# Seed stage of a two-layer network: three segments in turn instead of one, and no constant products

## The chip, the cores and the metric

The kernel runs on one core of a Trainium2 chip. The metric is device time in microseconds (us) for the whole program, from the first to the last instruction; lower is better. Times of before: 18684.27, 18656.47 and 18677.33 us, median 18677.33 us.

A core has five instruction queues that run side by side, each in its own order: TensorE (PE, matrix products into PSUM), VectorE (DVE), ScalarE (ACT, functions such as exp and silu), GpSimd (POOL) and SyncE (SP, which issues the transfers here). They meet only at semaphores: an instruction waits until what it reads is written and what it overwrites is read.

## The reference, cut to what matters

The reference is a network of two layers on 8 images of 128 channels and 64x64 points (L = 4096 points in a row). The change touches one part of the second layer: how `seed` comes from the layer's input.

```python
# per image; x is the first layer's result with the expert output added (x2 below)
v    = _ln_c(x)                                   # centre and scale over the channels
g    = einsum(v, seed_tok_w) + seed_tok_b         # 128 channels -> 8
gf   = _mamba(g.T, sm_in_w, in_b, conv_w, conv_b, A_log, D, dt_bias, rms_w, out_w, headdim=8, d_state=16) + g.T
seed = v + einsum(gf, seed_detok_w) + seed_detok_b
# _mamba: z, x, B, C, dt from one projection, a 3-tap convolution and silu;
# decay exp(cumsum(dt*A)) between any two points of a chunk; a state S handed from chunk to chunk;
# y*silu(z), divided by its root mean square, times out_w
```

The same normalised values, normalised once more, go to the other branch (`xs`), which the stage after this one (`cascade`) reads.

## The kernel before, in words

The program has, one after another, the first layer (until about 8.8 ms), its experts, a setup, the seed stage (`seeds`, L1457, from about 9.36 to 10.30 ms), the cascade (to about 17.1 ms) and the last feed-forward part. The seed stage alone is touched. The 8 images are worked together: their 8 x 8 tokens lie side by side on the partitions.

**Input units.** `seed_inputs` (L1359) is a generator with 64 units, one for each of 8 stretches of 512 points and 8 images. A unit goes through four steps, one at each `next`: `residual` (product `x2_p`, shown as `x_p` in the profile, then an addition and a store), `center` (product `ln_m`, a subtraction, a square), `scales` (product `ln_v`, three ACT functions, two DVE products, a store to `seed`) and `outputs` (two ACT functions, product `tok_p`, a store to `g_d`, a store to `xs`). So each `next` issues four products for four different units. All four take one of two PSUM banks with the tag "p".

**Segments.** The 4096 points are cut into 16 segments of 256 (SC). `seed_segment` (L1428) takes one through, with yields where other work may be put between:

- `tap_stack` (L1314) loads three shifted copies of `g_d` into one of two stacks `stk_sm`.
- `ssd_project` (L1079): products `bc_p`, `z_p`, `tok_p`; their silus on ACT between two loads of function tables; then softplus for dt, and in `ssd_exponents` (L1050) the cumulative-sum product `cs_p`, whose result is split in three bf16 parts, written to DRAM (`cs_sm`) and read back in 16 small transfers into the rows `ssA`, `ssB`; last `dec_p`, `cd_p` and `eA_p`.
- `ssd_chunk` (L1173), for each of two chunks of 128 points: `g_p`, masked into `gm`; two halves, each with four products `ss_p` of the rows, an exp into `E`, a DVE product with `gm`, and `y_p`; and the state S.
- `ssd_output` (L1291): square, product `ms_p`, Ln and exp, a POOL product, product `o_p`. Then `gf`, and for each image a product `det_p` (tag "p" again), a DVE addition `sd_x` and a store.

In the profile nearly all instructions have the line of a helper (L288 products, L296 ACT, L335 and L344 DVE or POOL), so names of tiles are followed, not lines. Products of the segment's own token projection are shown as `tok_p<-W_sm,stk_sm`, those of a unit as `tok_p<-xn,w_seeds`.

**Order.** `seeds` (L1473 to L1478) takes the segments one by one. It first draws enough units that the segment's stretch is in `g_d`, and then calls `next(ready)` once at every fourth yield of the segment, which has 20. Across the queues a scheduling layer of the language sets, when the program is built, the final order of each engine's instructions; it may move an instruction ahead of others as long as the data allow, and dependencies given by `self.after` hold as well. [...]

**Constant products.** `keep_warm` (L290) multiplies a constant tile by itself into a bank that the next product overwrites. Six of them stand ahead of `cs_p` (L1058) and six ahead of `ms_p` (L1300) in every segment of the seed stage; the cascade has none.

Of the kernel before, what the change touches and what calls it, by code (L numbers as in the profile page):

```python
# [9 lines left out]
F32 = mybir.dt.float32  # L10
BF16 = mybir.dt.bfloat16
AF = mybir.ActivationFunctionType
ALU = mybir.AluOpType
# [7 lines left out]
NB = 8  # L21
C = 128
# [256 lines left out]
class Net:  # L279
# [709 lines left out]
    def ssd_weights(self, pool, cfg, j):  # L989

        nc = self.nc
        n = f"{cfg.name}{j}"

        def part(i):
            o, m = self.at["stacked"][f"{n}_{i}"]
            return self.st[:, o : o + m]

        W = pool.tile([128, cfg.cols], F32, name=f"W_{n}")
        nc.vector.memset(W[96:], 0.0)
        self.tt(W[:KST], part(0), part(1), ALU.mult)  # L1000
        self.tt(W[:KST], W[:KST], part(2), ALU.add)
        negA = pool.tile([128, cfg.nh], F32, name=f"negA_{n}")
        self.act(negA, self.w(f"{n}_Alog"), AF.Exp)
        self.ts(negA, negA, -1.0, ALU.mult)
        D = pool.tile([128, cfg.g2, cfg.nh, cfg.hd], F32, name=f"D_{n}")
        for g in range(cfg.g2):
            nc.vector.tensor_copy(D[:, g], bc(self.w(f"{n}_D"), cfg.hd))
        wo = pool.tile([cfg.pz, cfg.gh * cfg.co], F32, name=f"wo_{n}")
        self.ts(wo, self.w(f"{n}_out")[: cfg.pz], self.w(f"{n}_rms")[: cfg.pz], ALU.mult)
        return {"W": W, "negA": negA, "D": D.rearrange("p g h q -> p (g h q)"), "wo": wo, "fill": 6 if cfg is SM else 0}  # L1010

    def ssd_rings(self, pool, cfg, n, npads, nrows, nstates):

        nc = self.nc
        pads = []
        for q in range(npads):
            t = pool.tile([128, cfg.g, cfg.pad], F32, name=f"pad_{cfg.name}{q}")
            nc.vector.memset(t, 0.0)  # L1020
            pads.append(t)
        ncs = n // 128 * (cfg.g // cfg.g4)
        rows_ = []
        for q in range(nrows):
            A = pool.tile([128, ncs, cfg.g4, 128], BF16, name=f"ssA_{cfg.name}{q}")
            for c in range(ncs):
                nc.vector.tensor_copy(A[:, c], bc(self.k("ss_one")[:, : cfg.g4], 128))
            B = pool.tile([128, ncs, cfg.nh, 128], BF16, name=f"ssB_{cfg.name}{q}")
            for c in range(ncs):
                nc.vector.tensor_copy(B[:, c], bc(self.k(f"ss_ind_{cfg.name}"), 128))  # L1030
            rows_.append((A, B))
        states = []
        for q in range(nstates):
            t = pool.tile([cfg.pb, cfg.np, cfg.g2 * cfg.hi], F32, name=f"Sd_{cfg.name}{q}")
            nc.vector.memset(t, 0.0)
            states.append(t)
        stacks = []
        for q in range(2):
            t = pool.tile([128, cfg.np, n], F32, name=f"stk_{cfg.name}{q}")
            nc.vector.memset(t[96:], 0.0)  # L1040
            stacks.append(t)
        return {"pads": pads, "rows": rows_, "states": states, "stacks": stacks,
                "pad": 0, "row": 0, "state": 0, "stack": 0}
# [6 lines left out]
    def ssd_exponents(self, cfg, dA, n_tok, ring, wk, ps, fill):  # L1050


        nc = self.nc
        NC, nh, G = n_tok // 128, cfg.nh, cfg.g
        n = NC * G * nh
        t_ = cfg.name
        p = ps.tile([128, S], F32, tag="b", bufs=self.narrow, name="cs_p")
        self.keep_warm(p, fill)  # L1058
        p = p[:n, :128]
        self.summed = self.mm(p, dA.rearrange("p c g -> p (c g)"), self.k("le"))  # L1060
        part = wk.tile([n, 3, 128], BF16, name=f"csq_{t_}")
        rest = wk.tile([n, 128], F32, name=f"csr_{t_}")
        nc.vector.tensor_copy(part[:, 0], p)
        self.tt(rest, p, part[:, 0], ALU.subtract)
        nc.vector.tensor_copy(part[:, 1], rest)
        self.tt(part[:, 2], rest, part[:, 1], ALU.subtract)
        d = self.dp.tile([3, n, 128], BF16, name=f"cs_{t_}", bufs=3)
        nc.sync.dma_start(d.rearrange("i n t -> n i t"), part)
        A, B = self.turn(ring, "row")
        g4 = cfg.g4  # L1070
        for r in range(g4):
            v = d.rearrange("i (c g h) t -> i c g h t", g=g4, h=nh)[:, :, r]
            nc.sync.dma_start(B[32 * r : 32 * r + 3], v)
            for i in range(3):
                o = 32 * r + 3 + i * nh
                nc.sync.dma_start(A[o : o + nh, :, r], v[i].rearrange("c h t -> h c t"))
        return A, B, part
# [213 lines left out]
    def ssd_output(self, cfg, W, sg, n_tok, wk, ps):  # L1291

        nc = self.nc
        NH, gh, pz, t_ = cfg.nhalf, cfg.gh, cfg.pz, cfg.name
        yz = sg["yz"]
        sq = wk.tile([pz, NH, n_tok], F32, name=f"sq_{t_}", bufs=1)
        self.act(sq, yz, AF.Square)
        yield None
        p = ps.tile([128, 2, S], F32, tag="a", bufs=self.wide, name="ms_p")
        self.keep_warm(p[:, 0], 6 if cfg is SM else 0)  # L1300
        for hf in range(NH):
            self.mm(p[:pz, hf, :n_tok], self.k(f"blk_{t_}")[:pz, :pz], sq[:, hf])
        self.rsqrt(sq, p[:pz, :NH, :n_tok], self.k("e5")[:pz])
        self.tt(yz, yz, sq, ALU.mult, nc.gpsimd)
        yield None
        o = ps.tile([128, S], F32, tag="b", bufs=self.narrow, name="o_p")
        n = gh * cfg.co
        for hf in range(NH):
            i = self.mm(o[hf * n : (hf + 1) * n, :n_tok], W["wo"], yz[:, hf])
            if cfg is CM and hf == 0:  # L1310
                self.after(i, self.projected)
        yield o[: NH * n, :n_tok]
# [46 lines left out]
    def seed_inputs(self, g_d, routed, wk, ps):  # L1359
# [16 lines left out]

        def residual(s, b, v):
            p = bank("x2_p")
            self.mm(p, self.eo[:, b, :], v["P"])
            self.tt(v["x"], v["x"], p, ALU.add)  # L1380
            nc.sync.dma_start(self.x2[b][:, v["sg"]], v["x"])

# [42 lines left out]
            made.pop(t - len(steps), None)  # L1425
            yield t - len(steps)

    def seed_segment(self, k, g_d, st, wk, ps):  # L1428

        nc = self.nc  # L1430
        sg = slice(k * SC, (k + 1) * SC)
        stk = self.tap_stack(g_d, k * SC, k == 0, st["ring"])
        xs = []
        for b in range(NB):
            x = wk.tile([C, SC], F32, name="sd_x", bufs=NB)
            nc.sync.dma_start(x, self.seed[b][:, sg])
            xs.append(x)
        for v in self.ssd_project(SM, self.ssw[2], st["ring"], lambda j: stk[:, j, :], SC, wk, ps):
            if v == "silu" or isinstance(v, dict):
                yield  # L1440
        for c in range(SC // 128):
            yield from self.ssd_chunk(SM, self.ssw[2], st, v, c, wk, ps)
        for o in self.ssd_output(SM, self.ssw[2], v, SC, wk, ps):
            if o is None:
                yield
        gf = self.gf[k % 2]
        for j in range(SM.np):
            self.tt(gf[32 * j : 32 * j + 32], o[32 * j : 32 * j + 32], stk[64:96, j, :], ALU.add)
        for b, x in enumerate(xs):
            p = ps.tile([C, S], F32, tag="p", bufs=2, name="det_p")  # L1450
            self.mm(p[:, :SC], self.w(f"detok_w{b}"), gf)
            self.stt(x, p[:, :SC], self.w("seed_detok_b"), x, ALU.add, ALU.add)
            nc.sync.dma_start(self.seed[b][:, sg], x)
            if b % 2:
                yield

    def seeds(self):  # L1457

        nc, tc = self.nc, self.tc
        with tc.tile_pool(name="sd", bufs=1) as pl, tc.tile_pool(name="sdw", bufs=2) as wk, \  # L1460
# [2 lines left out]
            self.weights(pl, "seeds")  # L1463
            self.silus_done([])
            g_d = self.dp.tile([8 * NB, L], F32, name="g_d")
            st = {"ring": self.ssd_rings(pl, SM, SC, 2, 2, 2), "S": None, "layer": 0}
            routed = [pl.tile([128, S], F32, name=f"P{q}") for q in range(3)]
            self.gf = [pl.tile([128, SC], F32, name=f"gf{q}") for q in range(2)]
            for z in routed + self.gf:
                nc.vector.memset(z[64:], 0.0)  # L1470
            ready = self.seed_inputs(g_d, routed, wk, ps)
            done = -1
            for k in range(NSC):  # L1473
                while done < (k * SC // S + 1) * NB - 1:
                    done = next(ready)
                for n, _ in enumerate(self.seed_segment(k, g_d, st, wk, ps)):
                    if n % 4 == 0:
                        done = next(ready, done)  # L1478
            self.wname, self.wt = second

    def cascade(self, ps):
# [410 lines left out]
```

## Time and profile before

| | us |
|---|---|
| median of three runs | 18677.33 |
| the profiled execution, time | 18687.58 |
| its span | 18685.8 |
| seed stage, first cumulative-sum product | 9441 |
| end of the part of the seed stage with input units | 10079 |
| last cumulative-sum product of the stage | 10256 |
| last `sd_x` addition of the stage | 10297 |

A row of the view by stretches gives, for each stretch of the span, how long each engine was busy, how many instructions it ran, and then the granted TensorE clock (PEclk, 1.00 is full), the share of transfer time and GB/s. A matmul counts as busy until its modelled end, so a PE that waits for its own pipeline is shown busy. A line of the view of waits reads: engine and what it was about to do, who released it, total us, times, longest. A line of the timeline reads: start, duration, engine, line, operation, output and inputs, count, and in brackets how long the engine had been idle and who ended it. Products in fp32 appear as two records each ("x2").

### The profile page before, as it was taken

The page shows a single profiled execution, that of the slowest core. Times are in us where ns is not written, and L with a number is a line of the kernel's source. Part 1 is how long each engine was busy: PE and PEld are TensorE (multiplying, and loading weights), DVE is VectorE, ACT ScalarE, POOL GpSimd, SP SyncE. Part 2 cuts the span into 40 slices and gives each one's busy share as a digit, 9 for nine tenths or more (in the row PEclk, how much of TensorE's full clock was granted, in tenths as well). Part 3 has the DMA queues.
Part 4 walks back from the last instruction along what each step waited for, and adds up shares of the span by engine and source line. Part 5 has one row for each costly group of instructions (what it writes and reads, how often), then busy time and mean ns, then how long its engine had stood idle before and what let it go on. Part 6 is the DMA issues. An engine that isn't in the chain of part 4 may idle for free. (4 is left out here: it accounts for less than half of the span.)

```text
span 18685.8 us, 299182 instructions
## 1 busy us (share of the span) xinstructions
PE 15883.7 (85%) x113284; PEld 8352.0 (45%) x114341; DVE 15169.7 (81%) x20453; ACT 11222.1 (60%) x15902; POOL 9320.4 (50%) x6308
## 2 busy tenths in 40 slices
PE   6877777777777777777777899999999999998898
PEld 2222222222222222222734577777777777774343
DVE  6999999999999999998355677777777777777886
ACT  5555656555565656554254577777767777776553
POOL 6777777777777777776011122222222222222444
PEclk8999999999999999999688999999999999998999
DMA  3555454545545455454443011111111111111222
GB/s 109 141 137 144 135 144 137 143 140 136 141 135 145 137 142 142 139 137 128 124 146 101 28 30 30 30 30 31 31 30 31 31 31 30 30 31 39 92 93 82
DMA packets 843742, 1734.87 MB, mean 93 GB/s; under 512 B 184315, under 2 KB 416667, under 8 KB 833883
## 3 DMA queue, kind: packets, MB, share of 16 engines
q1 hardware_dynamic: 842302, 1715.66, 32.3%
q8 instruction: 905, 14.83, 0.3%
q14 instruction: 535, 4.38, 0.1%
HBM read 1474.28 MB, written 241.04 MB: 92 GB/s over the span
## 5 line engine op out<-in xcount | busy, mean ns | idle before, releaser
L335 POOL TENSOR_TENSOR bx<-xE,B 128x1024 f32<-128x1024 f32 x2048 | 4821.7, 2358 | 998.5 <-DMA xE<-dtx_d 635.1
L288 PE MATMUL dA<-parts,expand 128*128 128x512 bf16 x11777 | 3152.5, 398 | 1868.7 <-DVE last L347 1376.5
L296 ACT ACTIVATE dA<-dA,negA 128x1024 f32<-128x1024 f32 x2048 | 2228.5, 1088 | 3199.2 <-PE dA L288 3085.9
L757 DVE TENSOR_TENSOR_SCAN dA<-dA,last,bx 128x1024 f32<-128x1024 f32 x1536 | 3609.3, 2350 | 92.3 <-POOL bx L335 69.5
L288 PEld LDWEIGHTS <-expand 128*128 128x128 bf16 x12288 | 1107.3, 100 | 4409.1 <-DVE last L347 2171.5
L344 DVE SCALAR_TENSOR_TENSOR E_cm<-E_cm,gm_cm 128x1024 f32<-128x1024 f32 x2048 | 2439.4, 1226 | 280.1 <-ACT E_cm L296 267.6
L335 DVE TENSOR_TENSOR hc<-dA,C 128x1024 f32<-128x1024 f32 x2048 | 2507.5, 1224 | 70.4
L1269 POOL COPY Sd_cm<-S_cm 64x128 f32<-64x128 f32 x1024 | 877.9, 857 | 2622.6 <-DVE S_cm L335 2533.2
L296 ACT ACTIVATE E_cm<-ss_p 128x1024 f32<-128x1024 f32 x2048 | 1981.6, 1021 | 265.6 <-PE ss_p L288 182.1
L335 POOL TENSOR_TENSOR xD_cm<-tok_cm,D_cm 128x256 f32<-128x256 f32 x512 | 403.9, 789 | 2375.0 <-PE y_p L288 2308.5
L288 PE MATMUL y_p<-E_cm,pad_cm 128*32 128x128 f32 x32768 | 1321.1, 277 | 119.1 <-DVE E_cm L344 118.2
L757 DVE TENSOR_TENSOR_SCAN dA<-dA,bx 128x1024 f32<-128x1024 f32 x512 | 1172.4, 2290 | 58.1 <-POOL bx L335 57.9
L288 PE MATMUL y<-hc,kt 128*32 128x512 f32 x8192 | 1200.8, 659 | 3.6 <-DVE hc L335 3.6
L288 PE MATMUL ss_p<-ssB_cm,ssA_cm 128*128 128x512 bf16 x3582 | 1040.2, 383 | 111.8 <-DVE gm_cm L335 43.2
L288 PEld LDWEIGHTS y_p<-E_cm,pad_cm 128*32 128x32 f32 x32768 | 903.7, 110 | 368.4 <-DVE E_cm L344 201.7
L288 PE MATMUL bc_p<-stk_cm,W_cm 128*128 128x256 f32 x4096 | 942.1, 383 | 25.2 <-DMA stk_cm<-xs 20.8
L1126 DVE COPY dtr_cm<-tok_p 128x16 f32<-128x16 f32 x1024 | 176.4, 172 | 865.2 <-ACT tok_cm L296 865.2
L288 PEld LDWEIGHTS bc_p<-stk_cm,W_cm 128*128 128x128 f32 x4096 | 770.1, 191 | 165.8 <-ACT E_cm L296 27.9
L288 PE MATMUL tok_p<-W_cm,stk_cm 128*128 128x200 f32 x4096 | 749.5, 336 | 0.0
L344 DVE SCALAR_TENSOR_TENSOR dw<-h,w_second,dw 128x512 f32<-128x512 f32 x1024 | 722.8, 747 | 1.4 <-ACT h L296 1.1
L296 ACT ACTIVATE tok_cm<-tok_p 128x384 f32<-128x384 f32 x1024 | 503.2, 491 | 345.4 <-DVE dtr_cm L1126 182.7
L288 PEld LDWEIGHTS tok_p<-W_cm,stk_cm 128*128 128x128 f32 x4096 | 683.1, 190 | 52.2 <-ACT BC_cm L296 48.5
(412 smaller groups left out, 29653.0 us busy)
## 6 DMA issues: line engine op xcount, KB each, us to landing
xE<-dtx_d SPq DMA_DIRECT2D x2048, 512.0 KB
dtx_d<-dtx SPq DMA_DIRECT2D x256, 256.0 KB
x<-x SPq DMA_DIRECT2D x256, 256.0 KB
pb<-p_d SPq DMA_DIRECT2D x64, 1024.0 KB
ssA_cm<-cs_cm SPq DMA_DIRECT2D x3072, 4.0 KB
stk_cm<-xs SPq DMA_DIRECT2D x368, 128.0 KB
stk_cm<-y SPq DMA_DIRECT2D x368, 128.0 KB
px<-in_x_dram SPq DMA_DIRECT2D x64, 256.0 KB
```

Source lines behind the costliest of these rows:

```text
L288: return self.ordered(self.nc.tensor.matmul(out, lhsT=lhsT, rhs=rhs, start=start, stop=stop))
L296: i = self.ordered(self.nc.scalar.activation(out, in_, func, **kw))
L335: self.ordered((eng or self.nc.vector).tensor_tensor(out, a, b, op))
L344: self.ordered(self.nc.vector.scalar_tensor_tensor(out=out, in0=a, scalar=s, in1=b, op0=op0, op1=op1))
L757: self.ordered(nc.vector.tensor_tensor_scan(out=t, data0=t, data1=bx.pop(n), initial=0.0 if ch["j"] == 0 else last[:, q : q + 1], op0=ALU. ...
L1126: nc.vector.tensor_copy(dtr[:, c, jj, :], v[:, :, cfg.wsil :])
L1269: nc.gpsimd.tensor_copy(Sd[gr, :, g * hi : (g + 1) * hi], S2[gr])
```

## The change

Segments are no longer taken through one by one. A turn handles three: the chunks of segment k, the projection of k+1 and the output of k-1, one step of each in turn, until all three are through; there are 18 turns for 16 segments. The projection draws two units right after its silus, and every sixth round of a turn (the first, seventh and thirteenth) draws one more. With `self.after(self.summed, self.routed)` the product `cs_p` must stand behind the last `x2_p` issued so far, so that the two units' products lie ahead of it in PE's queue. A third tap stack is added, since one is held from the projection to the output. The constant products go: `fill` is 0 for both configurations, and the call in `ssd_output` is removed.

```diff
-        return {"W": W, "negA": negA, "D": D.rearrange("p g h q -> p (g h q)"), "wo": wo, "fill": 6 if cfg is SM else 0}
+        return {"W": W, "negA": negA, "D": D.rearrange("p g h q -> p (g h q)"), "wo": wo, "fill": 0}
...
-        for q in range(2):
+        for q in range(3 if cfg is SM else 2):
             t = pool.tile([128, cfg.np, n], F32, name=f"stk_{cfg.name}{q}")
...
         self.summed = self.mm(p, dA.rearrange("p c g -> p (c g)"), self.k("le"))
+        if cfg is SM:
+            self.after(self.summed, self.routed)
...
         p = ps.tile([128, 2, S], F32, tag="a", bufs=self.wide, name="ms_p")
-        self.keep_warm(p[:, 0], 6 if cfg is SM else 0)
...
-            self.mm(p, self.eo[:, b, :], v["P"])
+            self.routed = self.mm(p, self.eo[:, b, :], v["P"])
...
-    def seed_segment(self, k, g_d, st, wk, ps):
...
-            for k in range(NSC):
-                while done < (k * SC // S + 1) * NB - 1:
-                    done = next(ready)
-                for n, _ in enumerate(self.seed_segment(k, g_d, st, wk, ps)):
-                    if n % 4 == 0:
-                        done = next(ready, done)
+            stk, seg = {}, {}
+
+            def project(k):
+                t = stk[k] = self.tap_stack(g_d, k * SC, k == 0, st["ring"])
+                for v in self.ssd_project(SM, W, st["ring"], lambda j: t[:, j, :], SC, wk, ps):
+                    if v == "silu":
+                        for _ in range(2):
+                            done[0] = next(ready, done[0])
+                    if v == "silu" or isinstance(v, dict):
+                        yield
+                seg[k] = v
+
+            def chunks(k):
+                for c in range(SC // 128):
+                    yield from self.ssd_chunk(SM, W, st, seg[k], c, wk, ps)
+                    yield
+
+            def output(k):
...
+                for o in self.ssd_output(SM, W, seg.pop(k), SC, wk, ps):
+                    if o is None:
+                        yield
+                gf, t = gfs[k % 2], stk.pop(k)
...
+                    if b % 2:
+                        yield
+
+            done = [-1]
+            for k in range(-1, NSC + 1):
+                while k + 1 < NSC and done[0] < ((k + 1) * SC // S + 1) * NB - 1:
+                    done[0] = next(ready)
+                gens = [g(i) for g, i in ((chunks, k), (project, k + 1), (output, k - 1)) if 0 <= i < NSC]
+                n = 0
+                while gens:
+                    for g in list(gens):
+                        if next(g, self) is self:
+                            gens.remove(g)
+                    n += 1
+                    if n % 6 == 1:
+                        done[0] = next(ready, done[0])
```

The bodies of `project`, `chunks` and `output` are those of `seed_segment`, with the same products, functions, additions and transfers.

More of the change, by code (lines that the diff above doesn't have):

```diff
@@ L1426, in seed_inputs @@
             yield t - len(steps)
-    def seed_segment(self, k, g_d, st, wk, ps):
[L1430 to L1455, printed above, removed]
     def seeds(self):
@@ L1465, in seeds @@
             g_d = self.dp.tile([8 * NB, L], F32, name="g_d")
+            W = self.ssw[2]
             st = {"ring": self.ssd_rings(pl, SM, SC, 2, 2, 2), "S": None, "layer": 0}
             routed = [pl.tile([128, S], F32, name=f"P{q}") for q in range(3)]
-            self.gf = [pl.tile([128, SC], F32, name=f"gf{q}") for q in range(2)]
-            for z in routed + self.gf:
+            gfs = [pl.tile([128, SC], F32, name=f"gf{q}") for q in range(2)]
+            for z in routed + gfs:
                 nc.vector.memset(z[64:], 0.0)
@@ L1471, in seeds @@
             ready = self.seed_inputs(g_d, routed, wk, ps)
-            done = -1
-            for k in range(NSC):
-                while done < (k * SC // S + 1) * NB - 1:
-                    done = next(ready)
-                for n, _ in enumerate(self.seed_segment(k, g_d, st, wk, ps)):
-                    if n % 4 == 0:
-                        done = next(ready, done)
+            stk, seg = {}, {}
[8 more added lines that the diff above has]
+                seg[k] = v
@@ new lines, in chunks @@
+            def chunks(k):
[3 more added lines that the diff above has]
+            def output(k):
+                sg = slice(k * SC, (k + 1) * SC)
+                xs = []
+                for b in range(NB):
+                    x = wk.tile([C, SC], F32, name="sd_x", bufs=NB)
+                    nc.sync.dma_start(x, self.seed[b][:, sg])
+                    xs.append(x)
+                for o in self.ssd_output(SM, W, seg.pop(k), SC, wk, ps):
+                    if o is None:
+                        yield
+                gf, t = gfs[k % 2], stk.pop(k)
+                for j in range(SM.np):
+                    self.tt(gf[32 * j : 32 * j + 32], o[32 * j : 32 * j + 32], t[64:96, j, :], ALU.add)
+                for b, x in enumerate(xs):
+                    p = ps.tile([C, S], F32, tag="p", bufs=2, name="det_p")
+                    self.mm(p[:, :SC], self.w(f"detok_w{b}"), gf)
+                    self.stt(x, p[:, :SC], self.w("seed_detok_b"), x, ALU.add, ALU.add)
+                    nc.sync.dma_start(self.seed[b][:, sg], x)
+                    if b % 2:
+                        yield
```

## The prediction

> **What bounds the kernel now.** I read the page first: no engine is full over the whole span, and the chain that ended last names no line of the seed stage, so its work must be read from its own stretch. I cut the stage at its cumulative-sum products: a head, ten segments with five input units each, one in which the units run out, four without units, and the tail.
>
> ```profile
> 9355.00:9441.00 86.00, 59.48 (x115) 20.71 (x115) 43.75 (x88) 51.11 (x82) 14.12 (x12) 0.84 0.52 164
> 9441.00:10028.00 587.00, 490.87 (x2779) 256.73 (x2798) 360.53 (x718) 343.58 (x562) 108.86 (x160) 0.92 0.45 143
> 10028.00:10079.00 51.00, 39.59 (x265) 21.94 (x265) 30.57 (x67) 28.87 (x47) 9.62 (x15) 0.93 0.31 105
> 10079.00:10256.00 177.00, 135.03 (x955) 89.80 (x962) 76.53 (x190) 52.76 (x84) 18.19 (x44) 0.73 0.17 52
> 10256.00:10300.00 44.00, 30.21 (x210) 18.69 (x210) 17.45 (x36) 6.79 (x10) 3.10 (x9) 0.65 0.09 30
> ```
>
> After the length come PE, weight loads, DVE, ACT, POOL, then clock, DMA share, GB/s. A segment with units takes 58.7 us, of which DVE works 36.1 and ACT 34.4; one without takes 44.2, DVE 19.1 and ACT 13.2. PE looks fuller than it is: a 512-column fp32 product starts its successor 0.86 us later, so five units cost 17 us and the segment's own products about 17. Nothing is full; the stage is a chain of handovers. The waits of the four segments without units say where:
>
> ```profile
> POOL yz_sm L335 <- ACT sq_sm L296: 81.3, 4, 20.8
> ACT E_sm L296 <- PE ss_p L288: 56.9, 8, 8.8
> DVE gf L335 <- PE o_p L288: 21.9, 4, 5.5
> PE cs_p L288 <- DVE dA_sm L335: 15.5, 4, 3.9
> ```
>
> ACT waits 14 us a segment for `ss_p`, and the timeline shows why: the rows go to DRAM and back first.
>
> ```profile
> 10211.18 0.41 PE L288 MATMUL cs_p<-kt,dA_sm 128*32 128x128 f32 x2 [3.87 <-DVE dA_sm L335]
> 10214.29 0.32 SPq L1068 DMA_DIRECT2D cs_sm<-csq_sm  x1
> 10223.40 1.87 PE L288 MATMUL ss_p<-ssB_sm,ssA_sm 128*128 128x256 bf16 x8 [0.87 <-DMA ssB_sm<-cs_sm]
> 10242.83 1.26 POOL L335 TENSOR_TENSOR yz_sm<-yz_sm,sq_sm 128x512 f32<-128x512 f32 x1 [20.45 <-ACT sq_sm L296]
> 10244.82 0.84 DVE L335 TENSOR_TENSOR gf<-o_p,stk_sm 32x256 f32<-32x256 f32 x2 [5.47 <-PE o_p L288]
> ```
>
> 12 us from sum to rows, and at the end 5.5 us in which DVE waits for the output's chain alone. The units have a rate of their own. In the head, where they run alone, the steps repeat every 5.47 us:
>
> ```profile
> 9389.41 0.68 ACT L296 ACTIVATE g<-tok_p,w_seeds 8x512 f32<-8x512 f32 x1 [0.54 <-PE tok_p L288]
> 9390.14 0.30 PEld L288 LDWEIGHTS ln_m<-x,kt 128*128 128x128 f32 x2 [0.74 <-ACT g L296]
> 9394.88 0.68 ACT L296 ACTIVATE g<-tok_p,w_seeds 8x512 f32<-8x512 f32 x1 [0.54 <-PE tok_p L288]
> ```
>
> That is four products through two banks, each waiting for ACT or DVE to empty one (`ln_m` for `g` here). Five units therefore need 27 us unless the rest fits around them.
>
> **The change, part by part.**
>
> *Constant products.* 192 go, 12 a segment.
>
> ```profile
> L288 PE MATMUL cs_p<-warm x80: 379/379/634, 9355.7 to 10251.1; 128*128 128x512 bf16 x80
> L288 PE MATMUL ms_p<-warm x80: 379/379/634, 9468.1 to 10280.3; 128*128 128x512 bf16 x80
> ```
>
> They start 0.22 us apart, 2.6 us a segment, almost all in PE's idle time: at most 1 us a segment is won. Their other effect is the clock, costed below.
>
> *Same work, new order.* Both built programs hold the same ACT, DVE, POOL and SP work but for one memset (0.49 us, once); no transfer is added, and the cascade's order is the same instruction for instruction. So the difference is the stage's length. Between neighbouring cumulative-sum products PE's new order holds 14 units before the first (12 before), then 3, 5 (without output), eight times 5, 2 with the units' remainder, one remainder, three times none, and a tail of three outputs. Let U be a turn with five units and F one without.
>
> *U, at full clock*, with durations of the trace, from `cs_p` at 0, in each engine's new order. (a) The output of k-1: `ms_p`, Ln 0.69 and exp 0.63 end at 4.2, POOL 1.26, `o_p` and `gf` (0.68 + 0.84) end at 7.3. DVE then has, in order, one product with E (1.22), eight `sd_x` (0.48) in pairs 1.35 us apart, `yy` and `yz` (0.42 each): 13.8. `det_p` and the units share the two banks, so the first unit's `tok_p` starts only at 13.5. Here ACT idles from 6 to 14.7. (b) First unit 5.9, to 19.4; second 7.0, to 26.4, since two E products precede its `xn` on DVE. (c) DVE first does two `gm` (0.69), pad and `xw` (0.4 each), then subtracts that unit's mean: 29.7; square, `ln_v`, third `ln_m`, subtraction, square: 33.8. (d) Table load 1.28, `bc_p`, its silu 1.02 ends at 37.1; `tok_p`, four silus of 0.38 with DVE copies between, load: 41.6. (e) Ln, Ln, exp, exp, E on ACT, E product and `xn` on DVE: 47.3. PE has idled 8 us. (f) The two units ordered ahead of `cs_p`: 5.2 and 5.0, to 57.4. The new wait costs here: dA is ready at 49.4, and `cs_p` stands behind the second `x2_p` until 57.4; queued behind it are `dec_p`, `ms_p` and all of (a), and DVE's `csq` and ACT's decays wait for it. Not the rows: they are needed a turn later, so the 12 us DRAM trip is hidden by a whole turn. SP issues 67 transfers a turn at about 0.4 us, 27 of 57 us; its stores wait in order for DVE, but the `P` and `x` loads queued behind them land some 5 us before use.
>
> *The clock.* About 15 us of U are products on that chain, so U = 57.4 + 15h with h the share of half clock. The trace's row gives 0.92 with units (h = 0.16): U = 59.8. Here a rule of the Trainium skill speaks against the change: "TensorE: Matmul & The Clock Gate", section "Why this matters for your kernels", says that a PE gap of more than about 3 us between bursts throws the clock back to half. The constant products filled such gaps, and the new turn has one of 8 us and one of 3. With two windows of 3.4 us (the page's figure, my estimate) lost after each, h = 0.23 and U = 60.8. The row agrees only in part: with twelve constant products a segment the clock was 0.73 in the segments without units, so they did not hold it. I take U = 61. Bounds: 55, if the unfilled pieces (a) and (d) overlap better than in my order, and 69 with h = 0.77.
>
> *F.* The same chain without units: output, eight `sd_x`, three E products: `cs_p` to last `y_p` 18.5; squares, load, silus, load, E, softplus to the next `cs_p` 13.1: 31.7. About 7 us are products; at the row's 0.73 (h = 0.54) 3.8 more: F = 35, bounds 32 and 38.
>
> *The sum.* Before: 9441.5 + 10 x 58.7 + 50.7 + 4 x 44.2 + 41.6 = 10297.6, the last `sd_x`. After: first `cs_p` 9448 (two units more, partly behind silus); 26 (silus 14, two units 11); U - 9 (no output, so units start at 4.5 instead of 13.5); 8 U; U - 8 (as before's 50.7 to 58.7); F + 2; 3 F; tail 56 (rest of chunk 14 with output 13, 18.5; chunk 15 with output 14, 20; output 15, 15.4 as before's last; 2 for the clock). Together 9515 + 10 U + 4 F = 9515 + 610 + 140 = 10265: 33 us less. The fixed parts win 19, F wins 37, U loses 23. The profiled execution (18687.6, span 18685.8) becomes 18655. It lay 10 us above the median of the runs, so I forecast 18677 - 33 = **18644 us**.
>
> **The rivals.** *Overlap works* (0.20): U = 55, F = 33; 10197, 18577 us. For it: ACT and DVE have 35 and 36 us a turn, and much of the new turn is slack. Against: order is fixed within a queue, and (a) and (e) hold units back behind DVE's and ACT's queues. *The clock falls* (0.20): without constant products most windows run at half, U = 69, F = 37.5; 10355, 18735 us. For it: 0.73 and 0.65 where PE is thin. Against: units alone, without constant products, keep clock 1.00 in the head from 9379 to 9433. It ends slower by over 0.2% (37 us) from U = 67.2 at F = 37. *Nothing gained* (0.15): the units' pace sets both, U = 63, F = 37; 10293, 18673 us. For it: only three late intervals are free of units.
>
> **How the numbers follow.** My forecast has 0.45, its own range 18620 to 18668. 0.2% or 37 us is about what the runs can tell from no change; the forecast sits just inside. Of its 0.45, 0.20 are faster and 0.25 same. Faster: 0.20 + 0.20 = 0.40; same: 0.25 + 0.15 = 0.40; slower 0.20. Range: half of each outer case left out, 18590 to 18735.
>
> **What would show it.** Eight intervals between cumulative-sum products near 61 us, three near 35; ACT idle before `g` about 9 us once a turn, behind `det_p`; `cs_p` released by PE's own order with dA ready 8 us before; clock near 0.88 with units; the wait of `E` for `ss_p` mostly gone. I am wrong if the five-unit turns fall under 58 or exceed 66, if the clock without units leaves 0.65 to 0.8, or if a transfer of the rows, `stk_sm` or `P` releases PE.

## The result, and the profile after

The changed kernel is slower by a small, sure amount: median 18693.44 us of 20 runs (18678.78 to 18744.02), beside 18672.33 us of 20 runs of the kernel before (18643.25 to 18712.92), ratio 1.0015 with a 95% interval of 1.0008 to 1.0022. By the ratio that is 28 us more (15 to 41); the medians lie 21 us apart. It is below the 0.2% that was called no change. The forecast was 33 us less.

The two profiled executions seem to say the opposite: span 18677.0 us after, 18685.8 before. But the change leaves the program outside the seed stage as it was, and in these two executions that part took 31 us less after than before (7.7 ahead of the stage, 23.4 behind it). The stage itself, from its first `x_p` to its last `sd_x`, runs from 9361.3 to 10296.5 before, 935.2 us, and from 9353.6 to 10311.1 after, 957.5 us: 22.3 us more, as the medians say. From here on stages are compared.

Here is the stage by stretches between cumulative-sum products (a turn runs from the copy `csq_sm` that reads one sum to the next such copy). The columns are length, then PE, weight loads, DVE, ACT, POOL, clock, DMA share, GB/s. The rows of after: head, first interval, second, the first turn with an output, seven more with five units each, the one in which the units run out, three without units and the one ahead of them, the tail.

```profile
9353.00:9440.00 87.00, 61.93 (x123) 21.30 (x123) 44.56 (x80) 57.80 (x93) 15.43 (x13) 0.92 0.56 177
9440.00:9474.00 34.00, 24.56 (x92) 12.04 (x92) 16.59 (x37) 22.37 (x40) 4.30 (x4) 0.85 0.37 114
9474.00:9524.00 50.00, 36.24 (x240) 18.05 (x238) 30.04 (x60) 32.76 (x54) 12.80 (x16) 0.93 0.44 133
9524.00:9597.00 73.00, 57.96 (x268) 30.12 (x268) 35.43 (x73) 34.71 (x57) 11.04 (x16) 0.74 0.35 109
9597.00:10034.00 437.00, 338.38 (x1878) 174.44 (x1877) 252.10 (x507) 242.17 (x394) 87.65 (x113) 0.88 0.43 136
10034.00:10085.00 51.00, 39.35 (x253) 22.05 (x253) 29.37 (x61) 26.24 (x43) 10.57 (x15) 0.90 0.31 103
10085.00:10246.00 161.00, 127.40 (x914) 84.08 (x914) 79.26 (x191) 55.54 (x90) 26.17 (x45) 0.77 0.20 62
10246.00:10312.00 66.00, 53.36 (x395) 33.51 (x394) 34.11 (x71) 13.02 (x18) 13.69 (x21) 0.73 0.25 79
```

DVE and ACT work as long per turn as before (36.0 and 34.6 us in a turn with units), so the time did not go to them. Seven of the turns took 61.1 to 64.4 us, but one, with the same instructions, took 72.9. What stands out beside its length is its clock, 0.74 instead of 0.84 to 0.89.

The timeline shows one turn's landmarks, in this order: ACT idle before the first unit's `g`, PE idle before the first unit after the silus, dA ready, and the cumulative-sum product.

```profile
9734.33 0.68 ACT L296 ACTIVATE g<-tok_p,w_seeds 8x512 f32<-8x512 f32 x1 [9.15 <-PE tok_p L288]
9768.67 2.08 PE L288 MATMUL tok_p<-xn,w_seeds 128*128 128x512 f32 x2 [6.61 <-DVE xn L335]
9770.78 0.18 DVE L335 TENSOR_TENSOR dA_sm<-dt_sm,negA_sm 128x32 f32<-128x32 f32 x1
9781.23 0.41 PE L288 MATMUL cs_p<-kt,dA_sm 128*32 128x128 f32 x2
```

Two more lines, of the waits between 10085 and 10246, where the units are gone:

```profile
ACT E_sm L296 <- PE ss_p L288: 63.7, 11, 17.4
PE cs_p L288 <- DVE dA_sm L335: 17.8, 4, 4.5
```

In each of these turns PE stands idle about 4.4 us while ACT loads the table of exp and works off softplus. Three such stretches and what followed each (same columns as the first table):

```profile
10118.40:10121.90 3.50, 0.45 (x4) 0.19 (x2) 1.35 (x3) 3.11 (x6) 0.00 (x0) 0.99 0.12 39
10121.90:10149.20 27.30, 24.89 (x128) 15.56 (x129) 10.19 (x28) 3.31 (x6) 3.02 (x6) 0.50 0.10 32
10162.80:10166.20 3.40, 0.00 (x0) 0.00 (x0) 1.53 (x4) 2.43 (x5) 0.00 (x0) 1.00 0.02 5
10166.20:10186.70 20.50, 18.68 (x109) 11.66 (x112) 6.99 (x20) 3.31 (x6) 3.02 (x6) 0.50 0.05 16
10203.80:10207.20 3.40, 0.00 (x0) 0.00 (x0) 1.70 (x4) 2.22 (x5) 0.00 (x0) 1.00 0.00 0
10207.20:10220.80 13.60, 11.99 (x84) 7.62 (x84) 5.35 (x15) 3.31 (x6) 2.29 (x5) 0.50 0.03 7
```

After 3.4 us with hardly a product, or none, the clock is at half for 27.3, 20.5 and 13.6 us, though PE is busy 88 to 91% of that time. The turns holding these times took 43.7, 40.8 and 37.8 us, in the same order.

### The profile page after: what moved, and what is told of

Read it like the earlier page. It is cut to its first block, busy times and chain, and to the rows that moved or that the text cites. A ratio compares the mean times of both kernels' runs of the same rounds, so it can differ in the third digit from the quotient of the medians.

```text
span 18677.0 us, 299873 instructions
## 1 busy us (share of the span) xinstructions
PE 15898.0 (85%) x114149; PEld 8325.9 (45%) x114149; DVE 15168.3 (81%) x20454; ACT 11224.3 (60%) x15902; POOL 9351.0 (50%) x6308
## 5 line engine op out<-in xcount | busy, mean ns | idle before, releaser
L288 PE MATMUL ss_p<-ssB_cm,ssA_cm 128*128 128x512 bf16 x4096 | 1088.4, 383 | 70.6 <-DVE gm_cm L335 44.0
```

The source lines that it names most:

```text
L288: return self.ordered(self.nc.tensor.matmul(out, lhsT=lhsT, rhs=rhs, start=start, stop=stop))
```

## The experiments

Theory A: PE's idle stretch, once a turn, lowers the clock, and far more of PE's work than I had counted lies on the path that sets a turn's length. Rivals: B, the waits set the time and the clock matters little; C, the removed constant products as such; D, the fixed order of the cumulative-sum product; E, the banks that output and units share.

All ratios are to runs of the kernel before on the same chip, whose median varied from 18666 to 18715 us from one chip or time to another. The stage, the turns and their clocks are of one profiled execution each; the one kernel that was profiled twice (e6, e10) gave stages 0.2 us apart. A clock in the table is the mean of its turns' clocks. "With units" are, in the new order, the eight turns with five units and an output, in the old order the first ten segments; "without" are the last three turns or four segments.

| kernel | ratio [95%] | stage us | with units, clock | without, clock |
|---|---|---|---|---|
| before | 1 | 935.2 | 58.7, 0.92 | 44.2, 0.73 |
| after | 1.0015 [1.0008, 1.0022] | 957.5 | 63.7, 0.87 | 40.8, 0.76 |
| e1 before, no constant products | 1.0007 [0.9999, 1.0015] | 950.1 | 59.7, 0.89 | 45.2, 0.64 |
| e2 after, constant products back | 1.0021 [1.0013, 1.0029] | 978.6 | 64.5, 0.91 | 45.1, 0.72 |
| e3 after, late stretches filled | 1.0001 [0.9992, 1.0009] | 939.1 | 63.4, 0.87 | 37.2, 0.85 |
| e4 after, order of `cs_p` free | 1.0029 [1.0020, 1.0039] | 977.3 | 67.2, 0.79 | 38.3, 0.82 |
| e5 after, all stretches filled | 0.9976 [0.9966, 0.9987] | 873.7 | 56.7, 0.96 | 35.3, 0.91 |
| e6 after, output in other banks | 0.9958 [0.9945, 0.9970] | 879.5 | 56.5, 0.91 | 36.6, 0.83 |
| e7 e5 and e6 together | 0.9959 [0.9947, 0.9972] | 848.8 | 54.6, 0.98 | 36.0, 0.82 |
| e8 before, stretch filled | 1.0009 [0.9999, 1.0018] | 944.7 | 58.5, 0.94 | 46.0, 0.73 |
| e9 before, output in other banks | 0.9972 [0.9961, 0.9983] | 869.8 | 52.3, 0.93 | 46.0, 0.70 |
| e10 as e6, again | 0.9971 [0.9962, 0.9980] | 879.7 | 56.6, 0.91 | 36.9, 0.82 |
| e11 as e9, no constant products | 0.9972 [0.9962, 0.9982] | 877.5 | 52.9, 0.91 | 45.0, 0.63 |
| e12 e6, late stretches filled | 0.9964 [0.9950, 0.9977] | 868.6 | 56.6, 0.91 | 34.9, 0.87 |

**e1, the removal alone.**

```diff
-"fill": 6 if cfg is SM else 0}
+"fill": 0}
-        self.keep_warm(p[:, 0], 6 if cfg is SM else 0)
```

> The kernel before, with only its 192 constant products taken out (both counts set to 0); its order otherwise as the planner then makes it. Theory A (PE's idle stretch at the table load and softplus sets the clock, and about half of PE's work lies on the chain): the constant products broke up part of that stretch, so without them the clock falls from 0.92 to about 0.88 in segments with units and from 0.73 to about 0.68 without, segments grow from 58.7 to about 60.5 and from 44.2 to about 45.5: some 23 us slower than before, near 18695. Theory B (the clock matters little, the waits set the time): up to 1 us a segment is won, 18656 to 18672. Theory C (the new order is at fault and not the removal): within 5 us of before.

The clock fell as theory A said, by its rows of ten segments with units and four without:

```profile
9452.00:10049.00 597.00, 487.76 (x2681) 260.07 (x2681) 360.56 (x719) 343.22 (x562) 108.80 (x160) 0.89 0.43 141
10102.00:10282.00 180.00, 135.66 (x911) 95.44 (x912) 75.74 (x187) 53.16 (x84) 18.20 (x44) 0.64 0.16 51
```

A segment with units grew by 1.0 us, one without by 1.0, the stage by 15; the ratio by 0.07%, which its interval does not tell from nothing. In the profiled stage the removal won nothing: where I had given it up to 1 us a segment, it cost about as much. PE's wait ahead of `cs_p` without units was 3.9 us before and is 4.1 here, so the constant products had not filled that stretch, though the prediction says so; how they held the clock is not shown.

**e2, the constant products back in the new order.**

```diff
-"fill": 0}
+"fill": 6 if cfg is SM else 0}
+        self.keep_warm(p[:, 0], 6 if cfg is SM else 0)
```

> The changed kernel, with the 192 constant products back at their two old places. In the program they now stand before the silus' products and before the mean of squares, not in the idle stretch before the cumulative sum. Theory A (only work inside the stretch helps): clock without units stays between 0.69 and 0.81, turns as after or up to 2 us longer, 18690 to 18720. Theory C (the constant products as such hold the clock, wherever they stand): clock near 0.92 with units, turns near 60.5 and 37, 18665 or less.

No faster than after: 1.0021 (the two intervals overlap), and the profiled stage is 21 us longer. So theory C alone doesn't hold. In the new order these products stand where PE has work to do, not in its idle stretch; without units the clock stays at 0.72, and those turns grew by 4.3 us, more than theory A allowed. But the planner shifted other instructions too when they came back, and turns alternated between 62.3 and 67.5 us, so this run doesn't price the products alone. With e1 it shows, by one profiled stage each, that the two parts of the change don't add: stage 935.2 (old order, with), 950.1 (old, without), 978.6 (new, with), 957.5 (new, without). By this the new order costs 7 us where there are no constant products, and 43 where there are.

**e3, sixteen constant products in the idle stretch, late turns only.** They are ordered behind the last `ss_p`, so they run where PE would wait. The program's turns with units are those of after.

```diff
-        self.keep_warm(p, fill)
+        for _ in range(0 if cfg is not SM else 0 if self.unit < NS * NB - 1 else 16):
+            i = self.mm(p, self.warm[:, :128], self.warm)
+            self.after(i, getattr(self, "decayed", self.projected))
```

(`decayed` is set to each `ss_p` product, `unit` to the number of each unit's first product.)

> The changed kernel, with 16 constant products put into PE's idle stretch just before the cumulative-sum product, only in the five turns from the one where the units run out (3.5 us of a stretch of 4.5 at full clock); all turns before stay in the same order. Theory A: the clock of those turns rises from 0.69 to 0.84 to about 0.95, turns without units from 43.7, 40.8, 37.8 to 31 to 33 each, the tail from 65 to about 58: 30 to 40 us less than after, 18655 to 18665. Theory B: clock or not, the turns stay at 38 to 44, or grow by up to 3 us where the constant products run at half clock: 18690 to 18705.

The wait of `cs_p` for dA fell from 17.8 us to 4.1, and the clock of the turns without units and of the tail rose from 0.77 and 0.73 to these:

```profile
PE cs_p L288 <- DVE dA_sm L335: 4.1, 4, 1.1
```

```profile
10159.00:10196.00 37.00, 32.56 (x244) 21.01 (x244) 18.82 (x48) 13.01 (x21) 5.11 (x11) 0.86 0.20 62
10196.00:10234.00 38.00, 33.90 (x243) 21.81 (x244) 18.85 (x47) 12.97 (x21) 5.12 (x11) 0.82 0.19 60
10234.00:10270.00 36.00, 31.89 (x241) 20.57 (x241) 18.61 (x47) 13.01 (x21) 5.12 (x11) 0.86 0.20 63
10270.00:10327.00 57.00, 45.69 (x396) 28.77 (x396) 33.75 (x70) 12.80 (x18) 11.69 (x21) 0.85 0.27 87
```

The turns went from 43.7, 40.8 and 37.8 to 36.9, 38.1 and 36.6, the tail from 64.9 to 56.6: 19 us together. The ratio fell from 1.0015 to 1.0001, some 26 us (the intervals just meet), though 80 more products run. Work that computes nothing made the kernel faster by raising the clock: theory B falls for these turns. The turns stayed over the 31 to 33 expected, because the clock came only to 0.85.

The turns with units, untouched here, give a first price of the clock. Those of after and of this run are 16 executions of the same instructions, in the same order but for one `x_p` in two turns of each run. They are between 61.1 and 72.9 us long, at clocks from 0.89 to 0.74. With h = 2 x (1 - clock) as the share of time at half clock, the line through them is 54.3 + 34.6 h, and none lies further than 1.5 us from it. Most of them lie at h of 0.22 to 0.32, so the slope hangs on the longest (29.8 without it), and the line says little of full clock. (A long turn can also lower its clock. The late turns of this run turn the argument round: there the clock was raised, and the length followed.) For the three turns of after without units the line is 28.9 + 24.4 h.

**e4, the cumulative-sum product free.**

```diff
-        if cfg is SM:
-            self.after(self.summed, self.routed)
```

> The changed kernel without the fixed order of the cumulative-sum product behind the units' last product; the planner then puts it ahead of the last two units' ends. Theory D (the fixed order is the cost: the cumulative sum is ready to start 8 us before it runs, and all behind it waits): turns with units fall from 62.4 to 56 to 58, 40 to 60 us less than after, 18635 to 18655. Theory A: what moves is only which work fills which hole, the idle stretch and its half clock stay: turns within 2 us of 62.4, 18675 to 18710.

Theory D falls as a forecast, with the wrong sign: 1.0029, at best level with after. The planner put `cs_p` two units earlier, but the eight turns with units grew to 67.2 us each, at a clock of 0.78 to 0.79:

```profile
9550.00:10088.00 538.00, 424.02 (x2146) 220.84 (x2144) 284.81 (x577) 269.43 (x449) 97.83 (x128) 0.78 0.39 126
```

At a like clock they are about 2 us shorter than those of the fixed order: 64.9 at 0.82 beside 67.0 in e3, 70.6 at 0.73 beside 72.9 in after. So the free order saves about 2 us a turn in itself and loses 5 to 6 to the clock. Of the 10 us between dA and `cs_p` that the trace of after shows (9770.96 to 9781.23), no more than this was to be won; why the clock fell is not shown.

**e5, all stretches filled.** As e3, with 24 constant products in turns with units.

```diff
+        for _ in range(0 if cfg is not SM else 24 if self.unit < NS * NB - 1 else 16):
```

> The changed kernel with constant products in the idle stretch of every turn: 24 (5.2 us at full clock, of a stretch of 6.6) in turns with units, 16 in the others. Theory A (the stretch lowers the clock, and a turn with units costs 53.8 + 36.5 h, h the share of half clock, as the turns of after and of the run with late filling lie on one line): clock from 0.89 to about 0.95, turns with units from 62.4 to 56 to 58, turns without near 37: some 60 us less than after, 18625 to 18640. Rival (the constant products delay the units that follow them, and the planner moves units about): turns with units stay at 61 to 65, 18670 to 18700.

```profile
9573.00:10027.00 454.00, 398.75 (x2328) 208.67 (x2336) 278.58 (x579) 271.27 (x449) 114.31 (x129) 0.96 0.47 149
```

These are the eight turns with units: clock 0.96, and each 53.1 (at 1.00) to 60.7 us, 56.7 in the mean. The kernel is 0.24% faster than before and 0.39% faster than after. The planner also moved units and other products against the stretch in alternate turns, and these turns are the shorter ones (53.1 to 55.1 beside 58.9 to 60.7), so not all of it is the clock. The stretch itself, PE waiting for the unit's `xn` behind ACT's table load, shrank from 46.4 us in seven turns to 6.7:

```profile
PE tok_p L288 <- DVE xn L335: 46.4, 7, 6.6
```

```profile
PE tok_p L288 <- DVE xn L335: 6.7, 7, 1.5
```

(first after, then this run).

**e6, the output's products in other banks.**

```diff
-                p = ps.tile([C, S], F32, tag="p", bufs=2, name="det_p")
+                p = ps.tile([C, S], F32, tag="b", bufs=self.narrow, name="det_p")
```

> The changed kernel with the output's eight products through the two banks of the chunk's sums instead of the two banks of the units, no constant products. Theory E (the units stand behind the output in its banks, so ACT idles 9 us a turn): a unit runs beside the output, the idle time of ACT before g falls from 9 to under 4 us, turns with units fall to 57 to 59, 18650 to 18665. Theory A: the idle stretch at softplus stays and with it the clock near 0.88; turns within 2 us of 62.4 and 18675 to 18710.

The largest gain of all single edits: 0.42% under before, 0.57% under after, with no product added (0.29 and 0.44% in its repeat, e10). The lines are the wait of `g` in seven turns with units, after and then here, and the stretch of all eight here:

```profile
ACT g L296 <- PE tok_p L288: 86.3, 27, 9.2
```

```profile
ACT g L296 <- PE tok_p L288: 24.2, 33, 2.1
9571.00:10023.00 452.00, 353.54 (x2145) 184.81 (x2144) 285.95 (x576) 278.72 (x448) 102.10 (x128) 0.91 0.47 149
```

A unit now runs beside the output, as theory E says: the turn is 56.5 us at 0.91, where the line of the shared banks gives 60.5 at that clock. Theory A's forecast for this run, no gain, was wrong. The idle stretch at softplus is still there (45.6 us in seven turns), and only part of the gain is clock.

**e7, both.** The edits of e5 and e6 together.

> The two before together: constant products in every idle stretch (24 with units, 16 without) and the output's products through the chunk's banks. If both theories hold the gains add: turns with units 53 to 56, 18590 to 18620. If only the clock counts, as with filling alone, 18625 to 18640.

The profiled stage is the shortest of all, 848.8 us, at a clock of 0.98 with units, but that execution was the fastest of five (18625.7); by the medians it is level with e6 alone. Whether the gains add stays open: the stage is 31 us shorter than that of e6, and with five runs of each the intervals reach some 24 us either way.

**e8, the stretch of the old order filled.** Sixteen constant products ahead of its `cs_p`, ordered behind the projection's last product.

```diff
-        self.keep_warm(p, fill)
+        for _ in range(fill):                      # fill 16
+            i = self.mm(p, self.warm[:, :128], self.warm)
+            self.after(i, self.projected)
```

> The kernel before with the constant products ahead of its cumulative-sum product raised from 6 to 16 and ordered behind the projection's last product, so that they lie in the idle stretch instead of ahead of the output's products; the six ahead of the mean of squares stay. Theory A holds for the old order too, with a smaller slope (segments with units lie near 54.5 + 25 h): clock without units from 0.73 to about 0.85 and those segments from 44.2 to about 41, segments with units from 58.7 to about 57.5: 20 to 25 us less than before, near 18645. If the old order does not feel the clock: within 8 us of before.

```profile
10080.00:10265.00 185.00, 148.70 (x996) 95.43 (x1004) 77.55 (x192) 52.73 (x84) 18.21 (x44) 0.72 0.16 51
PE cs_p L288 <- DVE dA_sm L335: 5.1, 5, 2.6
10126.30:10129.70 3.40, 2.53 (x25) 1.88 (x26) 2.69 (x13) 0.38 (x2) 0.00 (x0) 1.00 0.45 131
10129.70:10153.60 23.90, 18.46 (x144) 12.01 (x148) 9.27 (x15) 4.47 (x5) 1.84 (x8) 0.50 0.02 4
```

Wrong: the stretch was filled (PE's wait for dA fell from 15.5 us to 5.1), but the clock of the segments without units stayed at 0.72, and they grew by 1.8 us. Behind each of the last five `cs_p` the clock still fell to half for 23.9 us, 1.8 to 3.1 us after its start; the last two rows are one such place. Four of the five times PE had not been idle for more than 0.63 us at a stretch in the 10 us before. So an idle stretch of over 3 us is not the only thing that lowers the clock; what lowers it here stays open.

**e9, the other banks in the old order.** The edit of e6 in `seed_segment`.

> The kernel before, constant products kept, with only the output's eight products moved from the units' two banks to the two banks of the chunk's sums. If the gain of that move belongs to the new order (there a unit stood 9 us behind the output, here ACT waits for g at most 5 us), the old order gains little: segments with units 57.5 to 58.5, within 0.1% of before. If the shared banks cost the same in both orders, segments with units fall by 4 to 6 us and the run is 0.2 to 0.35% faster than before.

The second of the two expectations held. The old order gains as much: segments with units from 58.7 to 52.3 us, ratio 0.9972. Here too units queued behind the output, in some four waits a segment of up to 5.4 us:

```profile
ACT g L296 <- PE tok_p L288: 93.8, 36, 5.4
```

```profile
ACT g L296 <- PE tok_p L288: 45.9, 44, 1.7
```

(before, nine segments; then this run, nine segments). So the shared banks held back both kernels and do not explain why the new one is slower.

**e10, e11, the two orders side by side.** e10 is e6 again, e11 is e9 without constant products, both on one chip.

> The changed kernel with the output's products in the chunk's banks once more, beside the two runs below on one chip, so that the two orders stand side by side with the banks apart. If the new order is the worse one whatever the banks, it is 0.1 to 0.2% slower than the old order with banks apart and no constant products; if the order costs nothing once no unit waits behind the output, it is level with it or faster: stage near 880 us again.

> The kernel before with the output's products in the chunk's banks and without its constant products: what the run above is, but for the order. From the two parts alone: the bank move gave 0.28%, the constant products' removal cost 0.07%, together 0.2% under before. Segments with units near 53, without near 46.

Level: 0.9971 and 0.9972, stages 879.7 and 877.5. With the banks apart the new order loses 3.7 us in a turn with units (56.6 against 52.9) and wins 8.1 in one without (36.9 against 45.0); the tail, with three outputs to finish, is 60.2 against 41.0.

**e12, e6 with the late stretches filled.** The edits of e3 and e6.

> The changed kernel with the output's products in the chunk's banks and 16 constant products in the idle stretch of the turns without units. Theory A (the stretch's half clock there still costs): clock of these turns from 0.85 to over 0.9, turns from 36.5 to 34 or 35, tail from 60 to about 54, 10 to 15 us less than without. Rival (the constant products take up what they win): within 5 us of it.

Not settled: ratio 0.9964 against 0.9971 of e10, medians 18637.35 and 18637.22. The clock without units rose from 0.82 to 0.87 and the turns fell by 2.0 us, the tail by 1.9, too little for these intervals.

e6 and e9 each beat both kernels, by some 50 to 80 us of the time before. Which of them is better stays open.

## Why the prediction was wrong

Counted from the same point (the start of the stage, 7.7 us earlier after), the sum missed by 54 us: the last `sd_x` lies at 10318.8 instead of 10265.

| term | forecast | measured | miss |
|---|---|---|---|
| first `cs_p` | 9448 | 9448.0 | 0 |
| first interval | 26 | 33.5 | +7.5 |
| second, U - 9 | 52 | 50.4 | -1.6 |
| first turn with an output | 61 | 72.9 | +11.9 |
| seven more turns U | 427 | 436.6 | +9.6 |
| U - 8 | 53 | 51.3 | -1.7 |
| F + 2 | 37 | 38.9 | +1.9 |
| three F | 105 | 122.3 | +17.3 |
| tail | 56 | 64.9 | +8.9 |

**Right: the clock itself.** With units I forecast 0.88, and seven of the eight turns had 0.84 to 0.89; without units I kept 0.73, and it was 0.70 to 0.82. The idle stretches stood where they were expected: 9.15 us before `g` behind `det_p`, 6.6 us before the first unit after the silus, dA ready well before `cs_p`, and `cs_p` released by PE's own order.

**Wrong: what the clock costs.** "About 15 us of U are products on that chain" and "About 7 us are products" of F are the steps that failed, as sizes of terms. I followed one chain through DVE, ACT and PE, counted the products that stood on it, and multiplied by h, as if the half clock fell evenly over the turn. It fell behind the idle stretch, where PE then has work queued: in the three turns without units it is busy 24.89, 18.68 and 11.99 us of those pieces (rows above). At half clock half of such time is lost: 12.4, 9.3 and 6.0 us, where I had allowed 3.8. Taken off the turns of 43.7, 40.8 and 37.8 us, it leaves 31.3, 31.5 and 31.8, which is the 31.7 that I had worked out for full clock. A late turn of e5 that ran at full clock throughout took 32.4. So the chain of F was counted right and only the price was too low. This is most of the 17 us of F; and in the tail 8.3 of the 8.9 us went in e3, where its clock rose from 0.72 to 0.85 (I had allowed 2 us for the clock there).

The turns with units fit the same reckoning. These are the half-clock pieces of the long turn, and the two of a usual one:

```profile
9524.50:9538.20 13.70, 13.69 (x90) 8.91 (x90) 5.41 (x14) 3.12 (x5) 3.02 (x6) 0.50 0.20 67
9555.20:9558.70 3.50, 3.33 (x22) 1.41 (x26) 2.07 (x6) 0.00 (x0) 0.00 (x0) 0.51 0.36 134
9562.10:9572.30 10.20, 8.82 (x14) 4.55 (x15) 1.38 (x2) 2.46 (x3) 0.00 (x0) 0.50 0.29 85
9579.10:9589.40 10.30, 5.49 (x6) 1.80 (x6) 5.39 (x11) 6.98 (x14) 2.58 (x2) 0.50 0.32 107
9746.40:9749.80 3.40, 3.40 (x15) 1.44 (x14) 2.63 (x7) 0.63 (x1) 0.00 (x0) 0.50 0.35 131
9763.50:9773.70 10.20, 5.03 (x6) 1.80 (x6) 5.15 (x10) 6.91 (x14) 2.58 (x2) 0.50 0.33 105
```

Half of PE's busy time in them is 15.7 us and 4.2 us; over the 16 turns of after and e3 what is left lies between 56.4 and 58.7 us, 57.6 in the mean, beside my 57.4. Here the price was a little too low in a usual turn (4.2 to 5.0 us for 3.5), and the larger part of the miss is two turns that spent 37.5 and 20.5 us at half clock instead of 13.7. I did not foresee that; what set it off there stays open.

The same sum over the whole stage, half of PE's busy time at half clock and then the rest, is an estimate from the traces, for it takes all of that time to lie on the path: before 105 and 830 us, e1 139 and 811, after 113 and 844, e3 94 and 845, e5 52 and 822, e6 71 and 809. Between after and e3 only the first part moves, by 19 us, as it should where little but the clock changes. By this the 22 us over before are some 8 of clock and 14 of everything else, and e5 owes 22 of its 84 us to the moved instructions.

**Wrong: the recovery.** I took "two windows of 3.4 us" lost after each gap, after the Trainium skill. "TensorE: Matmul & The Clock Gate", section "What's actually happening", has the full clock return after one busy window or more of that length. Here the idle stretch cost three such pieces in a usual turn with units and four, six and eight without, there with PE busy 88 to 91%. With units the total came out right by luck: my other gap cost one piece, and one and three make the four I had. Without units I had not used the rule but the old row's clock. Nor is a gap of over 3 us needed for a fall, as e8 shows.

**Wrong: a count.** "two units 11" of the first interval: three units' `g` lie in it (9441.4, 9459.3 and 9468.2), with the idle stretch among them. My own list of PE's order had three there.

**Wrong: that the removal wins up to 1 us a segment.** Alone it made the profiled stage about 1 us a segment longer (e1): by the estimate above it won 19 us of work and lost 34 to the clock. In the new order bringing the products back at their old places did not help (e2); where they stand decides (e3, e5).

**Overrated: step (f), "The new wait costs here".** Taken away, it gave about 2 us a turn at a like clock, and the clock took more than that back (e4).

**Half right: the wait of `E`.** It vanished with units (before from 9561 to 10028, after from 9597 to 10034):

```profile
ACT E_sm L296 <- PE ss_p L288: 33.3, 13, 5.1
ACT E_sm L296 <- PE ss_p L288: 1.4, 7, 0.2
```

Without them it grew from 56.9 to 63.7, in intervals that are shorter: the rows are there in time, but `ss_p` now stands behind `det_p` and `y_p` in PE's order. The turns without units did become shorter than the segments were, 40.8 for 44.2, by 3.4 us instead of the 9 counted on.

**Right, but unpriced: the shared banks of step (a).** I named them and put them down as fixed. They were worth 0.3% in the old order (e9) and 0.4 to 0.6% in the new (e6 and e10 against after), twice to four times the effect of the change.

Of the rivals, *Overlap works* is out. *Nothing gained* (18673) had the turn with units, 63, nearly right, but not the ones without. *The clock falls* (18735) named the lever, but by a clock mostly at half (h = 0.77), where it was a higher price at an h of 0.27. The result lies between the two.

## What to carry to other kernels

Before a reordering, price the clock from the trace: take the stretches at half clock and half of PE's busy time in them, instead of spreading a mean clock over the products on one chain; without units the price here was 1.6 to 3.3 times as high. Check it on turns of the same instructions at different clocks. A stretch of over 3 us in which PE has nothing to do can be followed by several times its length at half clock, so look at what fills it before taking filler work away, and put filler inside the stretch, not at a fixed place in the code; in the old order even that did nothing (e8), so try it before counting on it. And when two streams of work are to overlap, first see that they don't pass through the same PSUM banks: that one line was worth more than the whole change.

## What the runs showed of the hardware

After an idle piece of 3.4 us, half clock lasted 13.6, 20.5 and 27.3 us at 88 to 91% PE load, in turns of the same instructions (after); the length of the recovery is not fixed. The clock also fell to half where PE had not been idle for more than 0.63 us at a stretch (e8). The same turn took from 61.1 to 72.9 us at clocks from 0.89 to 0.74. Constant products raised the clock with units from 0.87 to 0.96 and shortened the stage by 84 us in the profiled executions, together with the instructions that moved (e5), while adding 3.5 to 5.2 us of PE work to a turn (16 or 24 of them, 0.22 us each).
